# Moving weight loads and row stores from ScalarE's to GpSimd's DMA queue in a four-layer convolution kernel

## The chip, the core and the metric

The kernel runs on one core of a Trainium2 chip. A core has five engines, each with its own instruction stream: TensorE (PE, matrix products), VectorE (DVE), ScalarE (ACT), GpSimd (POOL) and SyncE (SP). They meet only through semaphores. A DMA transfer is started by an instruction in the stream of SP, ACT or POOL, and is then carried out by DMA engines that all three share. An instruction that waits for a semaphore holds up everything behind it in its own stream, and that includes a DMA start.

The metric is the time of one execution on the device in microseconds (us), as a median over runs. Lower is better.

## The reference

The input is a batch of 8 images with 384 channels and 32 x 32 pixels, in 32-bit floating point. Four layers follow, each of the form x + layer(groupnorm(x)), with 32 groups of 12 channels:

- Layer 0: three depthwise 3x3 convolutions (for q, k and v), each with a batch normalisation and a Gelu and then a 384 x 384 product; attention over the 1024 pixels with 8 heads; an output product and a batch normalisation.
- Layer 1: a mixture of 4 experts, each a two-layer network on every pixel, weighted with gates from a softmax.
- Layer 2: a depthwise 7x7 convolution with mirrored edges, plus a bias.
- Layer 3: three branches. Each splits the channels into four chunks of 96; two chunks go through a small MLP (96 to 12 to 96 channels), the other two through a depthwise convolution of size 1, 3 or 5. The means of the branches give a softmax over the three, and the weighted sum goes through a 384 x 384 product.

```python
    # layer 3, one branch (chunks of 96 channels)
    h = _gelu(jnp.einsum('bchw,cd->bdhw', c, mw1[mi]) + mb1[mi][:, None, None])
    y = jnp.einsum('bdhw,dc->bchw', h, mw2[mi]) + mb2[mi][:, None, None]
```

## The kernel before

The channels are held as three tiles of 128 partitions. In most of the kernel the instructions of PE, ACT, DVE and POOL stand in the order of the program text (the blocks `tc.manual_schedule` with these engines); inside attention, which the diff doesn't touch, POOL is left to the compiler. Loads of data, issued by SP, are placed by the compiler.

**Depthwise convolutions as matrix products.** A depthwise convolution along the width is written as a banded 32 x 32 matrix for each channel and row of the filter, prepared on the host (`w0` for layer 0, `w7` for layer 2, `w35` and `w33` for layer 3). PE works with 64 x 64 quadrants, so two channels share a weight block. The bands come from DRAM into a tile `w`, and are then *spread* into a tile `wx` that is twice as wide: in each half one of the two channels is multiplied by one and the other by zero (`parity`). The convolution reads `wx`.

**Layer 0** (lines 451 to 580) has 36 groups: three channel tiles, three filters (q, k, v), four units. Group n's matmuls (line 530) read wx of group n. After them the text spreads the weights of group n+2 (`spread0`, line 481: ACT makes one half at line 486, POOL the other at line 487), starts the load for group n+3 (`weights_of`, line 475; `w` has three buffers, so it takes the buffer of group n), and has ACT copy the group's result out of PSUM (`evict_slots`, line 405). DVE transposes the results and takes their statistics (`results`, line 499), and SP stores them to DRAM. Before group 0 the text holds a group normalisation (`gn_coefs`; its power of -1/2 is POOL's, line 247), then the loads of groups 0 to 2, the spreads of groups 0 and 1, and the normalisation of the eight images on ACT (line 354) with DVE's transposes (line 468).

**Layer 2** (lines 1990 to 2041) has 3 x 8 steps of two halves each. A half is a call of `convolve7` (line 1112) followed by `next_weights` (line 1713), in which ACT spreads the weights of a half that comes three halves later (line 1725), and, after the second half of a tile, calls `load_weights` (line 1693) for a further one. Up to four loads are ahead of their spreads. In `load_weights` POOL adds the mirrored edge columns to a 7x7 tile after its load (line 1708), right behind the load in the text. The first loads of the layer, and two more at the change of memory pools, are issued by SP (`load_weights(nc.sync)`). The image results of a step are completed by DVE in `finish` (line 1844), which also has POOL copy edge pixels (line 1869).

**Layer 3** runs four convolutions in turn with `convolve3` (line 1952): unit 1 with 5x5 and 3x3, unit 0 with 5x5 and 3x3, eight steps each, again with `next_weights`; here two loads are ahead, and POOL adds nothing. Between the steps other jobs are inserted with `run` (line 1981):

- `hidden3(i)` (line 2158), i = 0 to 3: the first product of the MLPs for two images. `hidden_input` (line 1928) has POOL fetch two tiles of 512 KB for each image (line 1931, four `y` buffers in all), PE multiplies (line 2171), ACT applies the Gelu (line 2179), and the 72 rows `hid` of each image are stored to DRAM (line 2183). It is run before the 5x5 convolution of unit 0 and after its steps 0, 2 and 4. For i = 0 the fetches stand further up, in the 3x3 convolution of unit 1.
- `reorder` (line 1934), after step 5: POOL issues 48 DMAs of 128 KB that rearrange rows from DRAM to DRAM (line 1936).
- `branch_mean` and `branch_weights`, after steps 6 and 7: the softmax over the branches. Its factors go through DRAM with POOL's DMAs (lines 2251 to 2258).

The weights for the 3x3 convolution of unit 0 are requested from step 5 of the 5x5 one on. The projection (`project3`, line 2366) follows.

Of the kernel before, what the change touches and what calls it, by code (L numbers as in the profile page):

```python
# [175 lines left out]
def conv_mixer_kernel(ctx: ExitStack, tc: tile.TileContext, a: dict, out: bass.AP):  # L176
    nc = tc.nc
# [234 lines left out]
    with (  # L412
# [10 lines left out]
        for i in (0, 2):  # L423
            nc.gpsimd.tensor_tensor(
                out=b2s[:, :, i], in0=b2s[:, :, i], in1=b2s[:, :, i + 1], op=ALU.add
# [25 lines left out]
        with tc.tile_pool(name="cps", bufs=2, space=PSUM, reuse_waits="tile") as cps:  # L451
            xt0s = {}

            def prepare0(ct, b):

                if b == 0:
                    pool = cxb if ct == 1 else cxa
                    xt0s[ct] = pool.tile([P, 32, B, H + 2], FP, tag="xt0", name="xt0")
                    for row in (0, H + 1):
                        nc.gpsimd.memset(xt0s[ct][:, :, :, row : row + 1], 0.0)  # L460
                if ct == 0:
                    xn = x0[:, b]
                else:
                    xn = cy.tile([P, N], FP, tag="xn", name="xn")
                    nc.sync.dma_start(out=xn, in_=a["x"][b, :, ct, :])
                sx, tx = norms[ct]
                affine(xn, xn, sx[:, ct, b : b + 1], tx[:, ct, b : b + 1])
                nc.vector.transpose(  # L468
                    xt0s[ct][:, :, b, 1 : 1 + H].rearrange("p c h -> p h c"), img(xn)
                )  # L470

            groups = [(ct, v, u) for ct in range(NC) for v in VORDER for u in range(4)]
            weights0 = {}

            def weights_of(n):
                if n < len(groups):
                    w = cy.tile([P, 24, W], FP, tag="w", name="w")
                    nc.scalar.dma_start(out=w, in_=a["w0"][groups[n]])
                    weights0[n] = w

            def spread0(n):

                if n < len(groups):
                    w = weights0[n]
                    x = weights0[n] = cy.tile([P, 24, 2, W], FP, tag="wx", name="wx")
                    nc.scalar.activation(x[:, :, 0, :], w, AF.Copy, scale=parity[:, 0:1])
                    nc.gpsimd.tensor_scalar(x[:, :, 1, :], w, parity[:, 1:2], None, ALU.mult)

            def slot0():

                ps = cps.tile([P, 4, 2, B, H], FP, tag="ps", name="ps")
                return Slot(ps.rearrange("p i c b h -> p i (c b h)"))

            def stats2(b):
                xn = cy.tile([P, N], FP, tag="xn", name="xn")
                nc.sync.dma_start(out=xn, in_=a["x"][b, :, 2, :])
                x_stats(2, b, xn)

            def results(ct, v, b, o):
                y = cy.tile([P, N], FP, tag="y", name="y", bufs=4)  # L500
                nc.vector.transpose(img(y), o[:, b])
                bn_stats_of(stats[:, v * NC + ct, 2 * b : 2 * b + 2, :], y)
                nc.sync.dma_start(out=raw[v][b][:, ct, :], in_=y)

            def gelu0(v, ct):
                i, y = v * NC + ct, ys0[v][:, ct, :]
                affine(y, y, bn_s[:, i : i + 1], bn_t[:, i : i + 1], AF.Gelu)

            def coefs0(v):
                i = slice(v * NC, (v + 1) * NC)  # L510
                bn_coefs(stats[:, i], bn_gb[:, i], NC, bn_s[:, i], bn_t[:, i])

            for n in range(3):
                weights_of(n)
            for n in range(2):
                spread0(n)
            for b in range(B):
                prepare0(0, b)
            last_o, last = None, None
            for n, (ct, v, u) in enumerate(groups):  # L520
                if u == 0:

                    o = co.tile([P, B, H, 32], FP, tag="o", name="o")
                w = weights0.pop(n).rearrange("p r t w -> p r (t w)")
                ps = cps.tile([P, 4, 2, B, H], FP, tag="ps", name="ps")
                for cc in range(2):
                    for k in range(3):
                        for e, d, i in product(range(2), repeat=3):
                            r = slice(64 * i, 64 * i + 64)
                            nc.tensor.matmul(  # L530
                                ps[64 * d : 64 * d + 64, 2 * i + e, cc],
                                lhsT=w[r, 12 * cc + 6 * e + 3 * d + k, :],
                                rhs=xt0s[ct][r, 16 * d + 4 * u + 2 * e + cc, :, k : k + H],
                                start=k == 0, stop=k == 2,
                            )
                spread0(n + 2)
                weights_of(n + 3)
                m = n // 4
                if n < 2:
                    for b in range(4 * n, 4 * n + 4):  # L540
                        stats2(b)
                if n == 1:
                    norm = gn_steps((mvx[:, 0], mvx[:, 1]), slot0)
                    nc.gpsimd.dma_start(out=xstmem, in_=xst)
                    nc.vector.tensor_copy(gmx, next(norm))
                if n == 2:
                    norms[1] = norms[2] = next(norm)
                for b in {3: (0, 1), 4: (2, 3), 8: (4, 5), 9: (6,), 10: (7,)}.get(n, ()):
                    prepare0(1, b)
                if m in (3, 4, 5) and u < 2:  # L550
                    for b in ((0, 1), (2,), (3, 4), (5,), (6, 7), ())[2 * (m - 3) + u]:
                        prepare0(2, b)
                if (m, u) == (5, 3):
                    cxb_pool.close()
                    pp0 = pre_pool.enter_context(
                        tc.tile_pool(name="pre0", bufs=1, side="right", reuse_waits="tile")
                    )
                    pw = pp0.tile([P, 2, NC, NC, P], FP, tag="pw", name="pw")
                    for i, k in enumerate("qk"):
                        nc.sync.dma_start(out=pw[:, i], in_=a[f"pw_{k}"])  # L560
                if m > 0:
                    for b in ((0,), (1, 2), (3, 4), (5, 6, 7))[u]:
                        results(*last, b, last_o)
                before = VORDER[m % 3 - 1]
                if ct == NC - 1 and m % 3 and u == 1:
                    y0 = pp0.tile([P, NC, N], FP, tag=f"y{before}", name="y0")
                    nc.sync.dma_start(out=y0, in_=raw[before][0])
                    ys0[before] = y0
                if ct == NC - 1 and m % 3 and u == 3:
                    coefs0(before)  # L570
                evict_slots(o, ps, u)
                if m == 8 and u < 3:
                    gelu0(VORDER[0], u)
                if u == 3:
                    last, last_o = (ct, v), o
            for c in range(NC):
                gelu0(VORDER[1], c)
            for b in range(B):
                results(*last, b, last_o)
            coefs0(VORDER[2])  # L580
# [12 lines left out]
    def layers(again, early, xst, pre_pool, pp0, pw):  # L593
# [1096 lines left out]
        todo_load = [(K7, ct, c) for ct in range(NC) for c in range(8)]  # L1690
        todo_load += [(n, unit, c) for unit in (1, 0) for n in KS for c in range(8)]

        def load_weights(queue=nc.scalar):
            if not todo_load:
                return
            k, unit, c = todo_load.pop(0)
            rows, cols = 4 * k, W + (len(EDGE) if k == K7 else 0)
            n_loaded.append(c)
            if k == K7 and more_w and (len(n_loaded) - 4) % 4 > 1:
                w = more_w[0]()  # L1700
            else:
                w = late["lw"].tile([P, 4 * K7, W + len(EDGE)], FP, tag="w", name="w")
            w = w.rearrange("p r w -> p (r w)")[:, : rows * cols].rearrange("p (r w) -> p r w", w=cols)
            queue.dma_start(out=w, in_=a["w7" if k == K7 else f"w3{k}"][unit, c])
            if k == K7:
                for c0, e0 in ((0, W), (W - R7, W + R7)):
                    o = w[:, :, c0 : c0 + R7]
                    nc.gpsimd.tensor_tensor(out=o, in0=o, in1=w[:, :, e0 : e0 + R7], op=ALU.add)
            n = rows // WPARTS[k]
            for e in range(WPARTS[k]):  # L1710
                loaded.append(((k, unit, c, e), w[:, n * e : n * e + n, :W]))
# [278 lines left out]
        with tc.manual_schedule(engines=ORDERED | {mybir.EngineType.Pool}):  # L1990
# [167 lines left out]
            def hidden3(i):  # L2158
# [17 lines left out]
                for b in (2 * i, 2 * i + 1):  # L2176
                    hid = ty.tile([MR, N], FP, tag="r2", name="hid")
                    for h in range(2):
# [1 line left out]
                            hid[:, h * HF : (h + 1) * HF], units.pop(0), AF.Gelu,  # L2180
                            bias=hbias[:, b : b + 1], accum_out=hsum[:, b, h : h + 1],
                        )
                    nc.scalar.dma_start(out=hmem[b], in_=hid)

            hidden3(0)

# [385 lines left out]
```

## Time and profile before

| | us |
|---|---|
| median of 3 runs | 3132.24 (3130.01 to 3134.54) |
| the profiled execution | 3131.1 |
| its span, first to last instruction | 3129.4 |
| PE busy | 2978.0 (95%) |
| DVE busy | 1857.4 (59%) |
| ACT busy | 1211.5 (39%) |
| POOL busy | 858.7 (27%) |

By stage, from the busy times of the stretches:

| stretch, us | what | PE busy | DVE busy | ACT busy | POOL busy |
|---|---|---|---|---|---|
| 0 to 317 | layer 0 up to attention | 249 | 268 | 152 | 104 |
| 317 to 1728 | attention | 1402 | 666 | 645 | 36 |
| 1728 to 2625 | layer 1 | 890 | 671 | 220 | 645 |
| 2625 to 2821 | layer 2 | 164 | 100 | 85 | 28 |
| 2821 to 2991 | layer 3, convolutions and MLPs | 142 | 75 | 98 | 44 |
| 2991 to 3129 | layer 3, projection | 130 | 78 | 11 | 0 |

How to read the profile: a line of a timeline gives the start in us, the length in us, the engine, the line of the kernel, the operation, what it writes and reads with the shape, and how many such instructions were merged; in brackets, how long the engine was idle before it and what ended that idle time. ACTq, SPq and POOL with DMA_DIRECT2D are DMA starts. A wait row names the waiting engine and line, what it waited for, the total in us, how often, and the longest.

### The profile page before, as it was taken

What the parts mean: (1) busy time and instruction counts of PE and PEld (TensorE: products, weight loads), DVE (VectorE), ACT (ScalarE), POOL (GpSimd) and SP (SyncE); (2) the same over time, 40 slices, a digit from 0 to 9 for tenths busy, and PEclk for the clock granted to TensorE, in tenths of its full rate; (3) what the DMA queues carried; (4) which work ended last, traced back from release to release, by engine and by line L of the source; (5) the groups of instructions that cost most, each with busy time, mean ns of one, the idle gap of its engine ahead of it and who ended that gap; (6) DMA issues with size and microseconds to landing.
All of it is one profiled execution on the core that took longest, in us unless ns stands there. A gap on an engine that the chain in (4) does not pass through costs nothing. (4 is left out here: it accounts for less than half of the span.)

```text
span 3129.4 us, 45250 instructions
## 1 busy us (share of the span) xinstructions
PE 2978.0 (95%) x18280; PEld 1710.8 (55%) x18280; DVE 1857.4 (59%) x3066; ACT 1211.5 (39%) x1446; POOL 858.7 (27%) x1103
## 2 busy tenths in 40 slices
PE   4988999999999999999999999999999999886998
PEld 3765334343433434343433688788787877555543
DVE  6898344445454445444445777777777776457164
ACT  2655453544445353545433122222222223446520
POOL 2432000000000000000000577686777764111400
PEclk9999999999999999999999999999999999898999
DMA  6787102010111101110002111112112114967675
GB/s 220 262 281 287 57 23 83 23 63 23 61 46 41 63 23 63 44 63 23 31 23 94 74 41 65 57 49 85 45 45 81 52 37 161 335 204 251 232 227 187
DMA packets 89107, 323.03 MB, mean 103 GB/s; under 512 B 13608, under 2 KB 16000, under 8 KB 84664
## 3 DMA queue, kind: packets, MB, share of 16 engines
q1 hardware_dynamic: 64936, 251.71, 23.6%
q10 hardware_dynamic: 13776, 35.82, 3.7%
q0 software_dynamic: 10176, 32.51, 3.0%
q8 instruction: 146, 2.39, 0.3%
q14 instruction: 73, 0.60, 0.1%
HBM read 211.66 MB, written 111.68 MB: 103 GB/s over the span
## 5 line engine op out<-in xcount | busy, mean ns | idle before, releaser
L780 ACT ACTIVATE e<-sc 128x1024 f32<-128x1024 f32 x512 | 483.2, 1031 | 607.8 <-PE sc L773 607.7
L773 PE MATMUL sc<-qT,kT 64*128 64x512 f32 x2048 | 473.9, 602 | 0.0
L792 PE MATMUL av<-e,vT 128*64 128x512 f32 x2048 | 467.7, 599 | 0.0
L773 PEld LDWEIGHTS sc<-qT,kT 64*128 64x128 f32 x2048 | 186.8, 186 | 282.0 <-issue 231.3
L792 PEld LDWEIGHTS av<-e,vT 128*64 128x64 f32 x2048 | 135.5, 136 | 316.4 <-issue 316.4
L822 POOL DMA_DIRECT2D att<-att x45 | 23.7, 531 | 979.6 <-DVE att L817 979.6
L671 PE MATMUL sc<-y,pw 128*128 128x512 f32 x576 | 249.3, 594 | 0.0
L808 DVE LOAD_MASK_SELECT sm<-av x64 | 0.9, 14 | 417.0 <-PE av L792 417.0
L530 PE MATMUL ps<-xt,wx 64*64 64x256 f32 x3456 | 198.7, 388 | 35.2 <-DVE xt L468 20.1
L810 DVE RECIPROCAL inv<-sm 128x512 f32<-128x512 f32 x64 | 214.6, 3353 | 2.2
L1346 POOL TENSOR_TENSOR hs_sum<-hs,hs_sum 128x256 f32<-128x256 f32 (+1 forms) x225 | 209.7, 940 | 9.4
L1366 DVE TENSOR_TENSOR r<-r,p 128x256 f32<-128x256 f32 x416 | 153.2, 411 | 92.2 <-PE p L1357 90.7
L530 PEld LDWEIGHTS ps<-xt,wx 64*64 64x64 f32 x3456 | 156.8, 137 | 76.1 <-issue 39.7
L671 PEld LDWEIGHTS sc<-y,pw 128*128 128x128 f32 x576 | 108.8, 190 | 139.9 <-issue 138.5
L354 ACT ACTIVATE hs<-hs,b 128x512 f32<-128x512 f32 x135 | 88.4, 712 | 247.4 <-DVE hs L1308 246.8
L1116 PE MATMUL ps<-xt,wx 64*64 64x256 f32 (+1 forms) x2912 | 160.5, 379 | 23.8 <-ACT wx L1725 12.8
L1357 PE MATMUL p<-hs_sum,wsum 128*128 128x256 f32 x768 | 177.0, 384 | 0.0
L1308 DVE TENSOR_TENSOR hs<-p,hs_sum 128x256 f32<-128x256 f32 x270 | 114.5, 424 | 93.5 <-PE p L1299 39.0
L1299 PE MATMUL p<-forms,w 128*128 128x256 f32 x630 | 165.4, 379 | 0.0
L1323 PE MATMUL ph<-xn,w 128*128 128x512 f32 x342 | 159.3, 600 | 3.0 <-ACT xn L354 3.0
L1357 PEld LDWEIGHTS p<-hs_sum,wsum 128*128 128x128 f32 x768 | 149.2, 194 | 21.4
L1116 PEld LDWEIGHTS ps<-xt,wx 64*64 64x64 f32 x2912 | 109.2, 139 | 73.3 <-ACT wx L1725 15.1
(346 smaller groups left out, 4687.3 us busy)
## 6 DMA issues: line engine op xcount, KB each, us to landing
raw<-y SPq DMA_DIRECT2D x72, 512.0 KB
y<-raw SPq DMA_DIRECT2D x24, 1536.0 KB
x<-x SPq DMA_DIRECT2D x23, 608.0 KB
xt<-x SPq DMA_DIRECT2D x23, 608.0 KB
w<-in_w ACTq DMA_DIRECT2D x36, 384.0 KB
xn<-in_x SPq DMA_DIRECT2D x24, 512.0 KB
x<-in_x SPq DMA_DIRECT2D x16, 768.0 KB
z<-z POOLq DMA_DIRECT2D x16, 768.0 KB, 4.3
```

The lines of the kernel that those rows point to most:

```text
L530: nc.tensor.matmul(ps[64 * d : 64 * d + 64, 2 * i + e, cc], lhsT=w[r, 12 * cc + 6 * e + 3 * d + k, :], rhs=xt0s[ct][r, 16 * d + 4 * u + 2 ...
L671: nc.tensor.matmul(ps[:, h, :], lhsT=w[:, ct, pair, :], rhs=y[:, ct, h * HF : (h + 1) * HF], start=ct == 0, stop=ct == NC - 1,)
L773: nc.tensor.matmul(sc[:, s, :], lhsT=kTs[b][r, pair, m * P : (m + 1) * P], rhs=qTs[b][r, pair, h * HF : (h + 1) * HF], start=True, stop=True,)
L780: nc.scalar.activation(e, sc, AF.Exp, scale=1.0 if shifted else HD**-0.5)
L792: nc.tensor.matmul(av[64 * s : 64 * s + 64, :], lhsT=vTs[0][:, m, c0 : c0 + 64], rhs=e[:, s, :], start=m == 0, stop=m == N // P - 1,)
L810: nc.vector.reciprocal(inv, sm)
L1116: nc.tensor.matmul(ps[64 * d : 64 * d + 64, 2 * i + e, c % 2, images], lhsT=w[r, d * K7 + k, :], rhs=by_slot(xts[ct])[r, 16 * d + column(c ...
L1299: nc.tensor.matmul(ps[:, :QF], lhsT=block1(PRODUCTS[n][0])[:, e], rhs=form_of(n, xn), start=True, stop=True,)
L1323: nc.tensor.matmul(ph, lhsT=w1[:, e, ct, dc * P : (dc + 1) * P], rhs=xn[:, ct, :], start=ct == 0, stop=ct == NC - 1,)
L1346: eng.tensor_add(rows_of(o, hs, s), rows_of(i, hs, s), rows_of(j, hs, s))
L1357: nc.tensor.matmul(ps[:, :QF], lhsT=block(w)[:, e], rhs=rows_of(x, hs, e), start=e == 0, stop=e == E - 1,)
L1366: nc.vector.tensor_tensor(out=o, in0=o, in1=ps[:, :QF], op=op)
```

## The change

Three DMA starts move from ACT's stream to POOL's: the weight loads of layer 0 (36 of 384 KB), the weight loads of layers 2 and 3 that are not on SP (52 of 192 to 532 KB), and the stores of the MLPs' rows (8 of 288 KB). In layer 0 the load of group n+3 is also placed ahead of the spread of group n+2 in the text. Sizes, tiles, buffers and all arithmetic stay as they are.

```diff
             def weights_of(n):
                 if n < len(groups):
                     w = cy.tile([P, 24, W], FP, tag="w", name="w")
-                    nc.scalar.dma_start(out=w, in_=a["w0"][groups[n]])
+                    nc.gpsimd.dma_start(out=w, in_=a["w0"][groups[n]])
                     weights0[n] = w
...
+                weights_of(n + 3)
                 spread0(n + 2)
-                weights_of(n + 3)
                 m = n // 4
...
-        def load_weights(queue=nc.scalar):
+        def load_weights(queue=nc.gpsimd):
             if not todo_load:
                 return
...
-                    nc.scalar.dma_start(out=hmem[b], in_=hid)
+                    nc.gpsimd.dma_start(out=hmem[b], in_=hid)
```

## The prediction

> **What bounds the kernel now.** I read the table by stage first, then the waits inside the three stages that the change touches (layer 0, layer 2, layer 3). Attention and layer 1 (317 to 2625 us) keep TensorE (PE) 99% busy and hold no edited line, so a delay in layer 0 passes through them whole.
>
> Layer 0 first. In the busy time by stretch (length, then PE, weight loads, VectorE, ScalarE, GpSimd, clock, DMA share) VectorE (DVE) is busy 183 of 191 us:
>
> ```profile
> 84.00:275.00 191.00, 175.47 (x3130) 140.73 (x3123) 182.98 (x211) 108.56 (x83) 71.81 (x37) 0.98 0.84 288
> ```
>
> The DVE timeline shows its transposes and statistics back to back from 95 to 305 us with 2 us of idle. Before that comes a serial start: ScalarE (ACT) and GpSimd (POOL) timelines (start, length, engine, line):
>
> ```profile
> 28.34 1.30 ACTq L478 DMA_DIRECT2D w<-in_w  x3
> 33.33 1.91 ACT L486 ACTIVATE wx<-w,parity 128x768 f32<-128x768 f32 x2 [4.83 <-DMA w<-in_w]
> 37.34 2.37 ACT L354 ACTIVATE o<-o,gn_t,gn_s 128x1024 f32<-128x1024 f32 x2 [2.10 <-DVE gn_t L297]
> 34.15 2.94 POOL L247 TENSOR_TENSOR gn_s<-ve,mhalf 128x16 f32<-128x16 f32 x1 [9.05 <-DVE ve L246]
> ```
>
> Today the first loads land before ACT needs anything else; the normalisation at 37.34 waits only for POOL's power (L247).
>
> In layer 2 the waits (who, for whom, total us, times, longest) show ACT held by DMAs that have nothing to do with the tile it spreads:
>
> ```profile
> ACT wx L1725 <- DMA r<-r: 17.5, 2, 9.1
> ACT wx L1725 <- DMA y<-x: 11.1, 1, 11.1
> ACT wx L1725 <- DMA y<-y: 10.9, 1, 10.9
> ACT wx L1725 <- DMA fb<-in_fb: 10.2, 1, 10.2
> ```
>
> Each ends at an L1704 load on ACT's queue (2678.56, 2716.83, 2727.61, 2774.94, 2797.86 us). I read this as a load waiting for the completion of an earlier SP transfer whose semaphore it reuses; on POOL's queue the reordering DMAs show the same with a distance of eight. PE pays for it:
>
> ```profile
> 2718.57 8.78 PE L1116 MATMUL ps<-xt,wx 64*64 64x256 f32 x112 [4.56 <-ACT wx L1725]
> 2801.40 5.26 PE L1116 MATMUL ps<-xt,wx 64*64 64x256 f32 x56 [9.73 <-ACT o L405]
> ```
>
> In layer 3 POOL runs ahead of PE (POOL, PE and ACT timelines): the rows of the MLPs are fetched (L1931) while PE is still on the previous pair, and the reordering (L1936) begins 15 us before the last MLP ends on PE.
>
> ```profile
> 2887.03 0.54 POOL L1931 DMA_DIRECT2D y<-y  x1 [1.31 <-PE ps L2171]
> 2898.57 0.53 POOL L1931 DMA_DIRECT2D y<-y  x1 [6.73 <-PE ps L2171]
> 2919.34 3.01 POOL L1936 DMA_DIRECT2D ya<-y  x6
> 2952.26 0.50 POOL L1936 DMA_DIRECT2D ya<-y  x1 [3.35 <-issue]
> 2895.48 7.09 PE L2171 MATMUL ps<-y,mw1s 128*72 128x512 f32 x16
> 2927.38 7.09 PE L2171 MATMUL ps<-y,mw1s 128*72 128x512 f32 x16
> 2955.08 12.70 PE L1969 MATMUL ps<-xt,wx 64*64 64x256 f32 x192 [3.41 <-ACT o L405]
> 2905.89 0.30 ACTq L2183 DMA_DIRECT2D h<-hid  x1
> ```
>
> **The change part by part.** All three engines keep the order of the program text, so each moved DMA now waits its turn on POOL. ACT loses 36 + 44 + 8 issues of 0.33 us; they run beside its activations and I count nothing for them.
>
> *Layer 0.* The three first loads now stand behind POOL's power, which ends at 37.1 instead of allowing an issue at 28.34. No trace row has a 384 KB load on POOL; nearest are its 512 KB loads (5.1 us to landing) and ACT's own (4.9 us). With 5.0 the first tile is there at 42.1; two spreads (1.9 us) end at 44.0, and the normalisation moves from 37.34 to 44.0: +6.6 us. The Trainium skill ("DMA: Bandwidth & Descriptors", Anatomy of one DMA) fits 2.0 us + bytes/436e3, here 2.9 us, which would make it +4.5; I take the rows. The chain from there (8 transposes of 1.8 us, PE, the statistics, POOL's 4.2 us power) is serial, and DVE then never rests, so nothing is made up. The later loads, issued ahead of the spread and thus about one group earlier, shorten ACT's 32 us and POOL's 96 us of waits for w, and the 14 us that PE waits for ACT's evictions there; DVE hides that gain. It could return at most DVE's 2 us. Sum +6.6 (4.5 to 8).
>
> *Layer 2.* ACT is freed of foreign waits. PE's stalls before L1116 behind them are 3.52 + 4.56 + 1.98 + 2.45 + 9.73 = 22.2 us; after the two long ones the matmuls also run slow (granted clock 0.71 and 0.61; 112 in 8.78 and 56 in 5.26 us against 6.25 and 3.13), 4.6 us more. Ceiling 27 us. But on POOL a load is followed by its own edge addition (L1708), which waits for the landing, so the next load can't be issued before: one in flight instead of two or three. Today's mean from issue to addition over loads 7 to 22 is 5.8 us (3.7 to 8.5); with 0.75 for the additions and 0.5 for the issue that is 7.1 us per load, where a step of PE takes 6.25 and where today's pace with all stalls is 7.0. The eight edge copies (L1869) stand behind these additions, and the next image tiles wait for them. At 7.1 us the gain shrinks to about 3. With one in flight the landing should be shorter; at 5.0 us the chain runs 14 x 0.8 = 11 us ahead. I take -14 us (-3 to -27).
>
> *Layer 3, first part.* Sixteen loads of 320 and 192 KB come two at a time as before; ACT's 13 us of waits for w stay. Behind the fetches for the first MLP (POOL waits until 2871) and the power at 2876 to 2880, load 40 moves from 2878.2 to 2880.5; its tile is first used at 2890.95. Nothing.
>
> *Layer 3, the MLPs.* The stores of hid now stand on POOL between one pair's fetch and the next one's, and they wait for ACT's Gelu, which waits for PE. So a fetch can't start before the previous MLP is done:
> - Pair 1: second store at 2894.6, then two fw loads, 25 memsets, one weight load (together 3.2 us), two fetches (1.1), landing 5.0: 2903.4 instead of 2895.5: +7.9.
> - Pair 2: behind pair 1's stores (3.4 us after PE) and two weight loads, of which the second waits for ACT's spread after three quarters of the convolution between; fetches go out about 9.3 us after PE's MLP, land 14.5 after; the convolution between covers 9.0: +5.5. Pair 3 the same: +5.5.
> - Each gap costs a slow restart, by the row at 2801.40 about 2.1 us: 3 x 2.1 = 6.3.
>
> The third MLP thus ends at 2934.5 + 25.2 = 2959.7. Two stores and a weight load follow (5 us), and only then the 48 reordering DMAs: 2964.7 instead of 2919.34. They took 33.4 us; 48 x 0.50 = 24 is the floor. I take 29: until 2993.7. Behind them in the queue stand the weights of the last 3x3 convolution, loads 49 to 52. ACT waits for load 49 with its spread, in front of the eviction that PE needs at 2955.08: issue 0.5, landing 4.4, two spreads 2.2, eviction 1.9: 3002.7. That is +47 us (bounds 32, when fetches land in 3.5 us and the restart is free, and 58, with 33 us and landings of 6). The remaining loads 53 to 55 stand behind the factors' DMAs (4 to 5 us) and are in time. The projection after it (PE 130 of 138 us) shifts whole.
>
> **Sum.** Profiled execution 3131.1 us = span 3129.4 + 1.7. 3131.1 + 6.6 - 14 + 47 = 3170.7. The median of the runs is 1.1 higher: **about 3171 us**, +1.2%.
>
> **Rivals.**
> - *Faster* (chance 0.11): POOL's queue in layer 3 stays hidden. For it: today POOL waits there 27 us for PE and is busy 44 of 170 us. Against: those waits sit in the same order that the stores now enter. If the MLPs and the reordering cost nothing and layer 2 gives 22: 3132 + 6.6 - 22 = 3117. It decides from a layer-3 cost under 7 us.
> - *Layer 0 gains* (0.09): PE's 14 us behind ACT come back because DVE was only busy at the pace it was fed. Against: its 2 us of idle. Time 3171 - 20 = 3151.
> - *Starved loads* (0.07): the skill ("SBUF — State Buffer", SBUF: two separate sides) warns that descriptors of a GpSimd DMA can't be written while DVE holds the shared port, 0.62 becoming 3.1 us. At +2.5 us a load, the 14 serial ones of layer 2 cost 35, the start and three fetches 10: 3216. Against: today's some 140 issues on POOL take 0.50 to 0.75 us beside a busy DVE. I go by the rows.
> - *No effect* (0.05): gain and loss cancel, 3132.
>
> **How the numbers follow.** My case has 0.68, own range 3145 to 3196. A measurement of this kernel tells 0.2% (6.3 us) from no change. Slower 0.68 + 0.09 + 0.07 = 0.84, same 0.05, faster 0.11. The range reaches down to 3136, into the cancelling case, and leaves out the faster rival and most of the starved one.
>
> **What would show it.** Layer 0: POOL's first load near 37 us, PE's first L530 near 59 instead of 52.8. Layer 2: no ACT wait for r, y or fb; POOL waiting for w more than today's 110 us. Layer 3: gaps of 5 to 8 us before L2171, reordering from about 45 us later relative to the first MLP, and one PE gap near 30 us with ACT's spread waiting for w. The forecast is wrong if fetches of a pair still go out before the previous stores, or if the last convolution's weights are issued before the reordering.

## The result, and the profile after

| | before | after |
|---|---|---|
| median, us | 3132.49 (3130.01 to 3134.54, 4 runs) | 3164.95 (3163.34 to 3166.47, 4 runs) |
| ratio | | 1.0104, 95% interval 1.0086 to 1.0121 |
| span of the profiled execution | 3129.4 | 3162.9 |
| PE busy | 2978.0 | 2977.8 |
| POOL busy, instructions | 858.7, 1103 | 913.0, 1199 |

The kernel is 1.0% slower. PE does the same work, so its idle time grew by what the time grew. Three marks on PE's timeline cut the span into four stretches: S, the first L1116 (layer 2 begins); M, the first L2171 (the first MLP); K, the L1969 row with 192 matmuls (the last convolution begins); E, the end.

| stretch | before | after | difference |
|---|---|---|---|
| start to S | 2625.7 | 2632.3 | +6.6 |
| S to M: layer 2 and the first half of layer 3 | 258.2 | 242.1 | -16.2 |
| M to K: MLPs and reordering | 71.2 | 113.2 | +42.0 |
| K to E: last convolution, projection | 174.3 | 175.4 | +1.0 |
| span | 3129.4 | 3162.9 | +33.5 |

The rows of PE that stand at layer 0's first convolution, at S and at M, first before, then in the changed kernel:

```profile
52.83 13.00 PE L530 MATMUL ps<-xt,wx 64*64 64x256 f32 x192 [18.97 <-DVE xt L468]
2625.69 3.32 PE L1116 MATMUL ps<-xt,wx 64*64 64x128 f32 x112 [1.22 <-issue]
2883.93 7.09 PE L2171 MATMUL ps<-y,mw1s 128*72 128x512 f32 x16 [0.53 <-DVE mw1s L2165]
```

```profile
2632.31 3.33 PE L1116 MATMUL ps<-xt,wx 64*64 64x128 f32 x112 [1.22 <-issue]
2874.38 7.09 PE L2171 MATMUL ps<-y,mw1s 128*72 128x512 f32 x16 [1.49 <-DVE mw1s L2165]
```

The timeline of PE, changed kernel:

```profile
60.30 12.65 PE L530 MATMUL ps<-xt,wx 64*64 64x256 f32 x192 [24.94 <-DVE xt L468]
...
2670.41 67.83 PE L1116 MATMUL ps<-xt,wx 64*64 64x256 f32 x1232
2739.11 21.72 PE L1116 MATMUL ps<-xt,wx 64*64 64x256 f32 x392 [0.87 <-ACT wx L1725]
2765.88 18.20 PE L1116 MATMUL ps<-xt,wx 64*64 64x256 f32 x280 [5.05 <-ACT wx L1725]
2791.01 1.45 PE L279 MATMUL ps<-mv,gmatB 128*128 128x8 f32 x6 [6.61 <-DVE mv L1858]
2792.39 4.64 PE L1116 MATMUL ps<-xt,wx 64*64 64x256 f32 x56
...
2894.51 8.59 PE L2171 MATMUL ps<-y,mw1s 128*72 128x512 f32 x16 [8.50 <-DMA y<-y]
2916.68 1.95 PE L2171 MATMUL ps<-y,mw1s 128*72 128x512 f32 x2 [4.65 <-DMA y<-y]
2940.27 9.64 PE L2171 MATMUL ps<-y,mw1s 128*72 128x512 f32 x16 [4.95 <-DMA y<-y]
...
2987.54 13.48 PE L1969 MATMUL ps<-xt,wx 64*64 64x256 f32 x192 [20.41 <-ACT o L405]
```

The first convolution of layer 0 starts at 60.30 where it started at 52.83. Layer 2 no longer has the 9.73 us stall before its 56 matmuls; one of 5.05 is left of the others. Part of that saving is waited for just ahead, at L279: 6.61 us for DVE's statistics of the images, where before it was 1.35. Then three gaps stand before L2171 where there were none, and one of 20.41 where there was 3.41.

The timeline of POOL and two rows of ACT's, changed kernel:

```profile
38.56 1.71 POOL L478 DMA_DIRECT2D w<-in_w  x3
...
2904.92 0.54 POOL L2183 DMA_DIRECT2D h<-hid  x1 [14.93 <-ACT hid L2179]
...
2911.75 0.56 POOL L1704 DMA_DIRECT2D w<-in_w  x1 [4.03 <-ACT wx L1725]
2912.30 2.14 POOL L1931 DMA_DIRECT2D y<-y  x4
...
2954.48 9.59 POOL L1936 DMA_DIRECT2D ya<-y  x19
2965.53 14.28 POOL L1936 DMA_DIRECT2D ya<-y  x29 [1.46 <-DMA ya<-y]
2979.81 1.17 POOL L1704 DMA_DIRECT2D w<-in_w  x2
```

```profile
43.04 1.89 ACT L486 ACTIVATE wx<-w,parity 128x768 f32<-128x768 f32 x2 [12.03 <-DMA w<-in_w]
...
2983.61 2.13 ACT L1725 ACTIVATE wx<-w,parity 128x384 f32<-128x384 f32 x4 [22.84 <-DMA w<-in_w]
```

POOL sits 14.93 us before a store, then 4.03 before a weight load, and only then issues the four fetches of the next pair: PE waits for them at 2916.68. The reordering starts at 2954.48, and the weights of the last convolution go out behind its last DMA, at 2979.81; ACT has waited 22.84 us for them.

The waits of layer 2 (2600 to 2830), changed kernel:

```profile
POOL w L1708 <- DMA w<-in_w: 62.4, 13, 8.1
POOL xn L1708 <- DMA xn<-in_w: 42.9, 9, 8.2
POOL w L1704 <- ACT wx L1725: 30.9, 7, 8.4
ACT wx L1725 <- POOL w L1708: 30.4, 5, 15.7
```

ACT's waits for r, y and fb are gone. POOL waits for the landings as long as before (105 us against 110), but ACT's wait for the edge addition to the `w` tiles doubled, from 14.8 to 30.4 us.

### The profile page after: what moved, and what is told of

Same layout as the page of the kernel before. It is cut to its first block, busy times and chain, and to the rows that moved or that the text cites. A ratio compares the mean times of both kernels' runs of the same rounds, so it can differ in the third digit from the quotient of the medians.

```text
span 3162.9 us, 45335 instructions
## 1 busy us (share of the span) xinstructions
PE 2977.8 (94%) x18280; PEld 1710.9 (54%) x18280; DVE 1859.2 (59%) x3066; ACT 1208.2 (38%) x1446; POOL 913.0 (29%) x1199
## 5 line engine op out<-in xcount | busy, mean ns | idle before, releaser
L530 PE MATMUL ps<-xt,wx 64*64 64x256 f32 x3456 | 197.2, 388 | 41.7 <-DVE xt L468 24.9
L530 PEld LDWEIGHTS ps<-xt,wx 64*64 64x64 f32 x3456 | 154.1, 137 | 83.8 <-issue 35.1
L1116 PE MATMUL ps<-xt,wx 64*64 64x256 f32 (+1 forms) x2912 | 155.0, 371 | 7.1 <-ACT wx L1725 5.9
L1346 POOL TENSOR_TENSOR hs_sum<-hs 128x256 f32<-128x256 f32 (+1 forms) x135 | 133.0, 1014 | 58.8 <-ACT hs L354 50.5
```

Of the source, the lines that this page charges most:

```text
L530: nc.tensor.matmul(ps[64 * d : 64 * d + 64, 2 * i + e, cc], lhsT=w[r, 12 * cc + 6 * e + 3 * d + k, :], rhs=xt0s[ct][r, 16 * d + 4 * u + 2 ...
L1116: nc.tensor.matmul(ps[64 * d : 64 * d + 64, 2 * i + e, c % 2, images], lhsT=w[r, d * K7 + k, :], rhs=by_slot(xts[ct])[r, 16 * d + column(c ...
L1346: eng.tensor_add(rows_of(o, hs, s), rows_of(i, hs, s), rows_of(j, hs, s))
```

## The experiments

Each kernel's stretches come from its own profiled execution, its ratio from all its runs against those of before on the same chip. On those chips single executions of one kernel lie up to 10 us from the median, and S alone lies between 2629.4 and 2637.4 us in kernels with the same layer 0. So layers are compared by stretches, and totals by ratios.

| kernel | S | S to M | M to K | K to E | median, us | ratio to before (95%) |
|---|---|---|---|---|---|---|
| before | 2625.7 | 258.2 | 71.2 | 174.3 | | |
| after | 2632.3 | 242.1 | 113.2 | 175.4 | 3164.95 | 1.0104 (1.0086 to 1.0121) |
| layer 0 only | 2633.2 | 256.5 | 70.6 | 173.5 | 3136.37 | 1.0021 (1.0014 to 1.0028) |
| 7x7 loads only | 2625.5 | 250.9 | 70.6 | 174.3 | 3123.09 | 0.9978 (0.9969 to 0.9988) |
| layer 3's loads only | 2625.6 | 246.0 | 115.2 | 175.9 | 3163.98 | 1.0108 (1.0091 to 1.0125) |
| stores only | 2622.9 | 256.1 | 89.6 | 184.3 | 3160.70 | 1.0101 (1.0084 to 1.0119) |
| layer 0, first three on ACT | 2622.3 | 254.8 | 71.4 | 174.0 | 3131.45 | 0.9999 (0.9988 to 1.0009) |
| after, last 3x3 loads on ACT | 2633.6 | 243.1 | 96.3 | 183.9 | 3156.27 | 1.0073 (1.0051 to 1.0094) |
| 7x7 loads and one more | 2625.4 | 241.1 | 70.5 | 174.4 | 3115.34 | 0.9949 (0.9933 to 0.9965) |
| the same, addition put off | 2623.1 | 232.0 | 70.2 | 173.2 | 3107.16 | 0.9923 (0.9907 to 0.9940) |
| after, fetches on SP | 2632.3 | 242.7 | 95.6 | 178.3 | 3149.91 | 1.0061 (1.0042 to 1.0079) |
| after, reordering on SP | 2637.4 | 249.5 | 93.0 | 178.5 | 3153.79 | 1.0065 (1.0043 to 1.0087) |
| after, both on SP | 2629.4 | 245.2 | 74.6 | 180.1 | 3134.32 | 1.0010 (1.0001 to 1.0018) |
| after, both, and the rest mended | 2622.5 | 240.6 | 75.4 | 179.1 | 3120.85 | 0.9972 (0.9959 to 0.9986) |

### Layer 0 alone, and with its first loads left on ACT

The first kernel takes only layer 0's part of the change:

```diff
-                    nc.scalar.dma_start(out=w, in_=a["w0"][groups[n]])
+                    nc.gpsimd.dma_start(out=w, in_=a["w0"][groups[n]])
...
+                weights_of(n + 3)
                 spread0(n + 2)
-                weights_of(n + 3)
```

> Only the layer 0 loads move to GpSimd, each ahead of a spread; layers 2 and 3 as before. Theory (late start): the first three loads wait for the power and push the normalisation back; VectorE hides what the later loads gain, so +6.6 us (3138 to 3140), PE's first L530 6 to 8 us later, and the whole shift still there where attention begins. Rival (slower transfers on GpSimd's queue): the loss grows from group to group, L530 ends more than 10 us later and GpSimd waits longer for w. Rival (layer 0 gains): the 14 us that PE waits for evictions come back, 3120 to 3128.

It took 1.0021 of before, +6.6 us by the ratio. The second leaves the first three loads on ACT:

```diff
-                    nc.gpsimd.dma_start(out=w, in_=a["w0"][groups[n]])
+                    (nc.scalar if n < 3 else nc.gpsimd).dma_start(out=w, in_=a["w0"][groups[n]])
```

> Only layer 0 is changed, as in the run of layer 0 alone, but its first three loads stay on ScalarE; the later ones are issued by GpSimd ahead of the spread. Theory (the whole +6.6 us is the late start behind GpSimd's power, and VectorE's chain hides what earlier loads bring): the first L530 of TensorE at 52.8 to 53.5 as before, the first L1116 within 1 us of 2625.7, the time within 0.1% of before (3128 to 3130 on a chip where before takes 3129). Rival (layer 0 gains once the start is not late, since TensorE waited 14 us for ScalarE there): 5 to 14 us faster. Second rival (the later loads cost on GpSimd too): first L1116 3 us or more later.

Its first L530 starts at 52.18 us, and its time is that of before, 0.9999 with an interval of 0.11% either side. So the whole loss is tied to these three loads, and 33 loads moved and issued earlier bring nothing that can be measured: at most 3.8 us (0.12% of 3130).

### The 7x7 loads alone

```diff
+            queue = queue or (nc.gpsimd if k == K7 else nc.scalar)
             queue.dma_start(out=w, in_=a["w7" if k == K7 else f"w3{k}"][unit, c])
```

> Only the 7x7 weight loads of layer 2 move to GpSimd; the rest as before. Theory (foreign waits removed, then one load in flight): ScalarE's waits for r, y and fb before L1725 vanish, 14 to 17 us faster (3115 to 3119); what is left of PE's stalls is ScalarE waiting for GpSimd's additions. Rival (slower transfers): no gain or a loss, 3130 and above. Rival (full gain): all 27 us, 3105.

Only 0.9978, some 7 us instead of 14 to 17. Its PE timeline and its waits in layer 2 (its lines are one further down):

```profile
2793.90 5.33 PE L1116 MATMUL ps<-xt,wx 64*64 64x256 f32 x56 [10.49 <-ACT o L405]
```

```profile
ACT wx L1726 <- DMA y<-y: 18.5, 1, 18.5
```

The stalls earlier in layer 2 are gone, but the last and longest remains: ACT waits there 18.5 us for an SP transfer at the first load that is *not* 7x7, the first 5x5 load of layer 3, which this kernel leaves on ACT.

### The loads of layer 3 alone

```diff
+            queue = queue or (nc.scalar if k == K7 else nc.gpsimd)
```

> Only the weight loads of layer 3 move to GpSimd; the stores of hid stay on ScalarE. Theory as in the forecast (the stores hold the fetches): without them the fetches go out earlier, so gaps before L2171 of 2 to 4 us instead of 5 to 8, the reordering begins about 20 us earlier than with everything moved, and 15 to 25 us slower (3147 to 3157). Rival (the weight loads hold the fetches, since each waits for a spread that waits for a convolution on PE): gaps as large as with everything moved, reordering late by 35 us, 38 to 43 us slower (3170 to 3176).

1.0108: as slow as the whole change. Layer 2's last stall is gone although no 7x7 load moved, which agrees with the run before. M to K costs 44.0 us with all stores still on ACT. Its POOL and PE timelines:

```profile
2905.89 0.54 POOL L1705 DMA_DIRECT2D w<-in_w  x1 [18.57 <-ACT wx L1726]
2909.51 0.54 POOL L1705 DMA_DIRECT2D w<-in_w  x1 [3.08 <-ACT wx L1726]
2910.04 2.09 POOL L1932 DMA_DIRECT2D y<-y  x4
```

```profile
2986.73 12.11 PE L1970 MATMUL ps<-xt,wx 64*64 64x256 f32 x192 [23.10 <-ACT o L405]
```

A weight load needs a buffer that ACT's spread frees, and that spread stands behind the Gelus of the MLP. So a weight load alone holds the fetches behind it until the MLP is done, as a store would: 18.57 us here. PE waits 6.24, 4.47 and 4.38 us for the three pairs. The rival of the expectation was right.

### The stores alone

```diff
-                    nc.scalar.dma_start(out=hmem[b], in_=hid)
+                    nc.gpsimd.dma_start(out=hmem[b], in_=hid)
```

> Only the eight stores of hid move to GpSimd; all weight loads stay on ScalarE. Theory (the stores hold the fetches): a gap of about 6 us before the second L2171 group, none or under 2 us before the third and fourth, reordering begins 25 to 28 us later, and since the last 3x3 weights are on ScalarE only the factors behind the reordering delay the end: 15 to 20 us slower (3147 to 3153). Rival (weight loads hold them): under 8 us slower (below 3140).

1.0101, more than expected. Its PE timeline:

```profile
2898.39 9.85 PE L2171 MATMUL ps<-y,mw1s 128*72 128x512 f32 x16 [7.73 <-DMA y<-y]
2918.82 7.42 PE L2171 MATMUL ps<-y,mw1s 128*72 128x512 f32 x16 [1.66 <-DMA y<-y]
...
2968.61 12.44 PE L1969 MATMUL ps<-xt,wx 64*64 64x256 f32 x192 [2.84 <-ACT o L405]
...
2995.03 10.33 PE L1969 MATMUL ps<-xt,wx 64*64 64x256 f32 x144 [11.87 <-ACT o L405]
```

The gaps are shorter than with both moved (7.73, 1.66 and 1.76 + 1.77), and the weights, on ACT, are in time at 2968.61. But the reordering still starts behind the last stores, and the factors' DMAs stand behind it: ACT's scaling (L2316) waits 10.47 us for them, and PE 11.87 us for ACT. M to K costs 18.4 us and K to E 10.0. Loads alone cost 44 + 1.6 in these stretches, stores alone 28, both together 43: they hold the same queue at the same places, so their costs don't add.

### The changed kernel with the last loads back on ACT

```diff
+            queue = queue or (nc.scalar if (k, unit) == (3, 0) else nc.gpsimd)
```

> The changed kernel, but the eight loads of the 3x3 convolution of unit 0 (the last ones) are issued by ScalarE as before; all other moves stay. Theory of the prediction (the last 3x3 convolution waits for its weights behind the reordering): its gap before L1969, 20.4 us in the changed kernel, goes, and most of these 20 us come back: 3143 to 3150. Rival (the factors, whose DMAs stand behind the reordering as well, take the place of the weights, as the run with the stores alone suggests): TensorE then waits for ScalarE's scaling by the factors, about 12 us, near 2995, and only 5 to 10 us come back: 3152 to 3160.

1.0073 against 1.0104. Its PE timeline, and one row of ACT's:

```profile
2973.02 12.43 PE L1970 MATMUL ps<-xt,wx 64*64 64x256 f32 x192 [1.41 <-ACT o L405]
...
2997.75 9.86 PE L1970 MATMUL ps<-xt,wx 64*64 64x256 f32 x144 [10.20 <-ACT o L405]
```

```profile
2993.79 1.15 ACT L2317 ACTIVATE c<-c,factor 128x1024 f32<-128x1024 f32 x1 [9.14 <-DMA factor<-fmem]
```

The weights did stand behind the reordering: the gap of 20.41 falls to 1.41. But 8.5 us of the 16.9 saved come back at once, as a wait for the factors, as the rival said.

### The 7x7 loads and one more

```diff
+            queue = queue or (nc.gpsimd if k == K7 or (k, unit, c) == (5, 1, 0) else nc.scalar)
```

> The kernel before with the 7x7 loads of layer 2 and one more load, the first 5x5 one of layer 3, issued by GpSimd; layer 0, all other loads and the stores stay on ScalarE. Theory (the changed kernel's gain of 16 us in layer 2 has two parts: 7 from the 7x7 loads, 9 from ScalarE no longer waiting at the first 5x5 load for an earlier SyncE transfer): the stall of 9.7 us before the last 56 matmuls of L1116 goes, the first L1969 comes 15 to 17 us earlier, near 2805, layer 3 is as before: 3112 to 3115, faster than both kernels. Rival (the wait moves on to the next load that ScalarE issues, the second 5x5 one): 3119 to 3124, as with the 7x7 loads alone.

0.9949. One more load moved is worth another 0.3%: S to M is 241.1, as short as the changed kernel's 242.1, and layer 3 costs nothing. The wait did not pass on to the next load that ACT issues.

### Edge additions behind the next load

```diff
-            if k == K7:
-                for c0, e0 in ((0, W), (W - R7, W + R7)):
-                    o = w[:, :, c0 : c0 + R7]
-                    nc.gpsimd.tensor_tensor(out=o, in0=o, in1=w[:, :, e0 : e0 + R7], op=ALU.add)
+            flush()
+            if k == K7:
+                pending.append(((k, unit, c), w))
...
             key, w = loaded.pop(0)
+            if pending and pending[0][0] == key[:3]:
+                flush()
```

`flush` makes the addition of the load before, if it is still open.

> As the run with the 7x7 loads and the first 5x5 one on GpSimd, but each edge addition is put behind the issue of the next load in GpSimd's order, so that two loads are in flight instead of one. Theory of the prediction (one load in flight since the addition follows each load costs some of the gain): the wait of GpSimd for w before L1708 falls from 60 us to under 30, ScalarE's waits for L1708 (30 us) fall, and 1 to 5 us are gained on that run. Rival (the single load in flight is covered by TensorE's 6.25 us steps after the first few): within 1 us of that run. Second rival (the addition put off makes the spread wait longer): 2 us or more slower.

0.9923, the fastest of all and faster than both kernels: 8 us better than the run before by the medians, above the 1 to 5 expected. Without the edit POOL waited 54.3 us for w and 53.1 for xn; with it, the waits of layer 2 read:

```profile
POOL xn L1700 <- DMA xn<-in_w: 10.6, 8, 2.8
POOL w L1700 <- DMA w<-in_w: 10.1, 6, 3.5
```

Its PE timeline:

```profile
2661.12 104.73 PE L1116 MATMUL ps<-xt,wx 64*64 64x256 f32 x1904
2770.76 5.59 PE L1116 MATMUL ps<-xt,wx 64*64 64x256 f32 x56
```

POOL's 107 us of waiting for landings fall to 21, and 1904 matmuls run in one piece. S to M is 26.2 us shorter than before, where the prediction put the ceiling of layer 2 at 27.

### The changed kernel with fetches, reordering, or both on SP

SP issues nothing between 2861 and 3006 us in the changed kernel. The fetches of pairs 1 to 3 move there in the first kernel, the reordering in the second, both in the third:

```diff
-                nc.gpsimd.dma_start(out=ys[j], in_=y2mem[b][1 + j])
+                (nc.gpsimd if b < 2 else nc.sync).dma_start(out=ys[j], in_=y2mem[b][1 + j])
...
-                nc.gpsimd.dma_start(out=o.rearrange("d r n -> r d n"), in_=i.rearrange("d r n -> r d n"))
+                nc.sync.dma_start(out=o.rearrange("d r n -> r d n"), in_=i.rearrange("d r n -> r d n"))
```

> The changed kernel, but the rows of the second, third and fourth MLP pair are fetched by SyncE (which issues nothing between 2861 and 3006 us in the changed kernel) instead of GpSimd, so that they no longer stand behind the stores; the first pair's fetch, the stores, the weights and the reordering stay on GpSimd. Theory (the gaps before L2171 are the fetches standing behind the stores; they and their slow restarts are 8.5 + 4.7 + 5.0 + 6.4 = 24.5 us of layer 3's 43): the three gaps go, the reordering starts about 24 us earlier, and the end comes 20 to 25 us earlier: 3138 to 3143 where the changed kernel takes 3163. The gap of 20 us before L1969 behind the reordering stays. Rival (the gaps are not on the chain since the reordering, which waits for the stores, sets the end alone): under 8 us gained. Second rival (fetches on SyncE wait as long for their data or buffers): gaps stay.

1.0061: about 14 us of the changed kernel's cost came back, where 20 to 25 were expected. M to K fell by 17.6. Its PE timeline:

```profile
2891.79 9.31 PE L2172 MATMUL ps<-y,mw1s 128*72 128x512 f32 x16 [5.17 <-issue]
...
2970.55 12.83 PE L1970 MATMUL ps<-xt,wx 64*64 64x256 f32 x192 [20.35 <-ACT o L405]
```

The second and third gaps are gone (the rows at 2909.96 and 2925.91 wait for nothing), and the reordering starts 17 us earlier by the clock of the trace. The first gap stays, at 5.17 of 8.50 us, and not for the fetches: SP issued them from 2877.82 on, as early after the MLP's start as POOL did before, and they had landed by 2888. The rows of DVE and POOL show what PE waited for, the scaled weights `mw1s`:

```profile
2891.39 0.52 DVE L2166 TENSOR_TENSOR mw1s<-mw,s 128x144 f32<-128x144 f32 x2
```

```profile
DVE kcount L2139 <- POOL count L2121: 10.0, 1, 10.0
```

```profile
2887.87 0.88 POOL L2121 MEMSET count<- 128x1 f32 x25
```

DVE makes `mw1s` late because it stood 10.0 us at an earlier instruction that needs 25 small memsets of POOL. In the text these stand behind the first pair's two stores, of which POOL could issue the second only at 2886.24, when ACT's Gelu was done. Before, the memsets began 0.9 us after M and DVE did not wait for them; here they begin 12.9 us after it. With the loads alone moved DVE's wait for them was 2.9 us. So this gap belongs to the stores: a start that waits holds POOL's own instructions too, and through them DVE and PE.

> The changed kernel, but its 48 reordering DMAs (L1936) are issued by SyncE instead of GpSimd; fetches, stores and weights stay on GpSimd. Theory (the last convolution's weights and the factors stand behind 25 us of reordering on GpSimd): the reordering runs early on SyncE, the gap of 20.4 us before L1969 falls below 5, the three gaps before L2171 stay, and 16 to 21 us come back: 3142 to 3147 where the changed kernel takes 3163. Rival (without the reordering the weights and factors still come late, behind the stores alone): 8 to 12 us. Second rival (the reordering's transfers now run beside the fetches and delay them): gaps before L2171 grow by 3 us or more each.

1.0065. The gap before the last convolution falls from 20.41 to 0.93 us, and M to K by 20.2, as the theory said. But S to M is 7.4 longer and K to E 3.1 longer than in the changed kernel, so half of it is lost again.

> The changed kernel with both: fetches of the later pairs and the reordering issued by SyncE; the loads and stores stay on GpSimd. Theory (layer 3's cost of 43 us is the two orders on GpSimd's queue and nothing else; neither the stores nor the weight loads cost anything there by themselves): all of it comes back, 3119 to 3124, that is before + 6.6 of layer 0 - 16 of layer 2. Rival (a part of 10 us or more is another thing, such as issue on GpSimd being slower or the loads landing later there): 3130 or more.

1.0010: 29 us of the changed kernel's cost come back, not all 43. M to K is 74.6, within 3.4 of before, so the two orders on POOL's queue account for 38.6 of the 42.0 us of that stretch. What is left there is again the first gap (4.44 us, with DVE's wait of 9.3 for the memsets) and its slow restart (1.4), less 2.5 by which the gap before K is shorter than before. The rest that the expectation left out is in S to M (3.1 above the changed kernel) and in K to E (5.8 above before). Its PE timeline in that last stretch:

```profile
2949.19 10.80 PE L1970 MATMUL ps<-xt,wx 64*64 64x256 f32 x192 [0.93 <-ACT o L405]
...
2966.66 10.73 PE L1970 MATMUL ps<-xt,wx 64*64 64x256 f32 x144 [4.56 <-ACT o L405]
```

Two weight loads leave POOL at 2958.51, right behind the four factor DMAs; ACT waits 4.00 us for them, and PE 4.56 where it waited 1.75 before. What lengthens S to M in these two kernels is not settled. SP issues 25 of the reordering DMAs in the middle of layer 2 there too (from 2742.80 and from 2740.27 on), and PE's stall of 5.05 us grows to 7.57 and 7.71; no run shows whether the one causes the other.

### Everything mended at once

The kernel with both on SP, with layer 0's first three loads on ACT and the additions put off:

> As the run before, and besides layer 0's first three loads on ScalarE (which takes away the 6.6 us) and each edge addition behind the next load's issue (which gave 8 us more in layer 2): all moves of the change kept, with the queue orders that cost time mended. Theory (the effects add): 3119 to 3124 less 6.6 less 8, 3104 to 3110, as good as the best so far (0.9923 of before, 3107). Rival (with all loads on GpSimd, the edge additions that are put off also hold the 5x5 and 3x3 loads): 3112 or more.

0.9972, 14 us short of the best. Layer 2 is the reason. Its SP and PE timelines:

```profile
2732.87 19.07 SPq L1947 DMA_DIRECT2D ya<-y  x25
2752.04 0.53 SPq L1866 DMA_DIRECT2D y<-x  x1
```

```profile
2778.79 1.45 PE L279 MATMUL ps<-mv,gmatB 128*128 128x8 f32 x6 [13.23 <-DVE mv L1869]
```

And one of DVE's waits between 2740 and 2830:

```profile
DVE x L1863 <- DMA r<-r: 10.0, 1, 10.0
```

The 25 reordering DMAs that could start early stand 19 us in front of SP's next store of a finished image (L1866), which goes out at 2752.04 instead of 2742.95 in the best kernel. Behind it stands the fetch of the next image's residual r (2752.61 instead of 2743.33), and DVE waits 10.0 us for that where it waited 1.5 there. The images of the last step are late by as much: PE waits 13.23 us for their statistics where it waited 3.22, and S to M is 8.6 us longer. Moving the reordering to another queue moved its harm there too.

## Why the prediction was right, and where its steps were not

The forecast was 3171 us in a range of 3136 to 3196, slower with a chance of 0.84; measured was 3164.95. On the profiled executions the sum +6.6 - 14 + 47 stands against +6.6 - 16.2 + 43.0 (the last is M to K and K to E together).

**Layer 0, +6.6: right in size, and for the most part in cause.** The first load left POOL at 38.56, behind its power, and was there at 43.04, 4.5 us later, where 5.0 was taken. The row was nearer than the skill's fit ("DMA: Bandwidth & Descriptors", Anatomy of one DMA), which gives an estimate of 2.9 us. S moved by 6.62, and the kernel with only this part cost 6.6 by its ratio (4.4 to 8.8). But the power itself, which the step held at 37.1, ended at 38.59. Three image loads of SP, placed by the compiler, now start earlier, in one row before and after:

```profile
24.39 1.38 SPq L496 DMA_DIRECT2D xn<-in_x  x3
20.24 6.64 SPq L496 DMA_DIRECT2D xn<-in_x  x3
```

They are in transfer beside the small load that POOL's constants need: POOL waits 13.2 us for it instead of 10.8, and the power comes later:

```profile
35.65 2.94 POOL L247 TENSOR_TENSOR gn_s<-ve,mhalf 128x16 f32<-128x16 f32 x1 [8.05 <-DVE ve L246]
```

So 1.5 of the 7.5 us by which the first L530 starts later arise before POOL's power ends. The image loads start at 19.8 to 20.9 in every kernel with the three first loads on POOL, and at 24.16 in the one that leaves them on ACT, which loses nothing. "Nothing is made up" holds only roughly: DVE's last statistics before attention (L364) came 4.7 us later in the changed kernel and 7.4 with layer 0's part alone. That 6.6 was met to a tenth is partly luck. That DVE hides the gain of earlier loads holds as far as 0.12% can tell: the run with the first three loads left on ACT shows neither gain nor loss. So the rival in which layer 0 gains 20 us falls.

**Layer 2, -14: right in size, and right that two things pull.** The 14 was taken from between 3 and 27 and not worked out, so that 16.2 lies near it is partly luck. The ceiling of 27 us came out as 26.2 once two loads were in flight, and the single load in flight cost the difference, 9 us between the two kernels that differ in it. The place was left open: the step did not tell the 7x7 loads from the load at 2797.86, which is the first of layer 3. The 7x7 loads alone bring 7.3 of the 16.2 us; the stall of 9.7 us, which its ceiling counted, belonged to that one load. In "POOL waiting for w more than today's 110 us" the sign was wrong: POOL waited 105, and the price of the single load showed in ACT's wait for the addition instead. The cause assumed for ACT's foreign waits, a semaphore shared with an earlier SP transfer, is not shown: the runs say only that the wait went away with that one load and did not pass to the next.

**Layer 3, the MLPs, +47: right in mechanism, 4 too large.** The terms stand so:

| step | predicted | measured |
|---|---|---|
| gaps before L2171 | 7.9 + 5.5 + 5.5 = 18.9 | 8.5 + 4.65 + 4.95 = 18.1 |
| slow restarts, three | 6.3 | 1.5 + 2.6 + 2.55 = 6.7 |
| reordering begins, from M | 80.8 | 80.1 |
| reordering | 29 | 25.3 |
| from its end to K | 9.0 | 7.7 |
| M to K | 118.8 | 113.2 |

The restarts are the stretches of 16 L2171 matmuls (8.59, 9.7 and 9.64) less the 7.09 of before. The mis-sized term is the reordering: it ran at 0.53 us a DMA, almost at the floor of 24. Its DMAs landed 3.2 us after their issue in the median and POOL waited 1.5 us between them; before they took 4.4 us, and POOL waited eight times for an earlier one, 4.1 us in all (and once 3.35 for nothing that the profile shows). The gap before K was put near 30 and measured 20.41. Small slips of the working did not matter: 52 loads move in layers 2 and 3, not 44, at a price of nothing; the addends of pair 1 make 2903.9, not 2903.4; and a pair has four fetches (2.1 us), of which PE needs two first.

**The step that failed there** is its wording of the cause: "the stores of hid now stand on POOL between one pair's fetch and the next one's". That holds, but it is not what the cost hangs on. The bullet on pair 2 does name a weight load that waits for ACT's spread, but beside the stores and not as enough by itself. The weight loads of layer 3 without the stores cost all of it, the stores without the loads two thirds. Leaving the stores on ACT would have saved nothing. And the weights are not the only thing behind the reordering that sets the end: with them out of the way, the factors come 10 us late. "Loads 53 to 55 are in time" holds in the changed kernel only because everything else is late; with the reordering gone they were 4 us late. And the 25 memsets, which the step counted as time of POOL alone, hold DVE when a store stands in front of them: with the fetches out of the way that keeps 5.17 us of the first gap.

**The other rivals.** Starved loads: POOL's moved starts took 0.53 to 0.64 us and its 7x7 loads landed after 5.6 us in the median, against 5.8 from issue to addition before, so nothing of the 2.5 us a load is seen. Faster needed a layer-3 cost under 7 us; it was 43. No effect lay 33 us away.

## What to carry to other kernels

Before a DMA start is moved to another engine's queue, list what stands behind it there and what it waits for itself: a load that waits for its buffer holds that queue just as a store that waits for its data does, and one such start in front of a fetch is enough. List the engine's own instructions behind it as well: 25 memsets kept DVE and PE waiting here. Such costs are not a sum over the moved starts, so moving half of them back may save nothing; look for the part of the move whose queue is free (here the 7x7 loads and one more, with each addition behind the next load: 0.77% faster than before). And a stall need not belong to the stage it shows in: look for the instruction at which the waiting engine stands, even if it serves the next stage.

## What the hardware did that was not expected

- With two loads on POOL's queue in flight (mostly of 532 KB) one took 7.1 us from start to landing in the median (3.7 to 8.6), one at a time, without the later additions, 6.0 (3.8 to 8.5). Still two were better by 8 us in all, since the addition and the issue no longer lie between them.
- The same reordering DMAs (128 KB, DRAM to DRAM, rows permuted) occupied SP for 0.59 us each in the median and POOL for 0.50, although a plain load occupies SP for 0.32 and POOL for 0.54.
